# An LSTM with a residual on one core: GpSimd's output sums split in two, Strassen sums moved into the step, and the start of the x projection rewritten

## The chip, the cores and the metric

The kernel runs on one core of a Trainium2 chip. The metric is device time in microseconds (us) from the start of the program to its end. Five engines work side by side, each from its own queue, in the order in which the program lists its instructions: PE (TensorE, matrix products into PSUM), PEld (PE's loads of weights), DVE (VectorE), ACT (ScalarE) and POOL (GpSimd). SP starts DMAs. An engine waits for another by semaphores.

## The reference

The input x has 16 sequences of 512 steps with 512 features. The recurrence and the residual are:

```
xW = x @ Wx + b                        # Wx: 512 x 2048
a = xW[t] + h @ Wh                     # Wh: 512 x 2048, h0 given, c0 = 0
i, f, o = sigmoid(a[:512], a[512:1024], a[1024:1536]);  g = tanh(a[1536:])
c = f * c + i * g;   h = o * tanh(c)
out[:, t] = x[:, t] + h
```

All is in 32-bit floats; each of the 512 steps needs the h of the step before.

## The kernel before, in words

**Layout.** The four column blocks j of 32 units lie on the four groups of 32 partitions. A pair of steps q shares a tile: 32 columns are two steps of 16 sequences. The hidden units are two halves, a and b, with a PSUM bank each (`gates`, two per half, taken in turn by even and odd steps). Each loop step t computes `products` on PE, h @ Wh for the step, in 16-bit floats: Wh is three 16-bit pieces, wq0 to wq2, and h is stored in `parts` as a main part, a scaled remainder and their copies. STEP_PE lists the order: the digit is the piece, the first letter the half of h that is read, the second the half of the gates that is written. It is 96 matmuls of 256 columns in groups of four (one for each j). In one group of four the four run side by side.

**One step.** After its products, STEP gives the order of the small operations on DVE and ACT, for half a and half b: `turn` and `turno` (L378, a transpose from PSUM), `fold` and `foldo` (L385, adds the remainder's part), `act`, `sigo`, `scale` (ACT), `mix` (L417), `cell` (L423), `ctanh` (ACT, L427), then p1 (L444, the main part of the new h), h (L433, h itself into `hist`), rem (L452), p2 (L448) and p2r (L456, the remainders). q3 of STEP_PE needs p1 alone, q1 needs p2, q2 needs p2r. Two steps ahead, `seed` (L330, ACT) writes bias and x part from the bank `xb` into the gates of step t + 2, times a mask that selects the step of the pair.

**The x part.** It is made in two ways. For pairs q below 2*M0 (M0 = 6) `turn_x` (L218) transposes the x block into x^T and writes a half of it, `xH`; `project` (L226) multiplies by Wx in eight fp32 matmuls of 256 columns per chunk, with `xH` for the sigmoid gates' columns (the kernel uses tanh for a sigmoid, so these gates need a factor of 0.5) and x^T for the others. From m = M0 on, four steps at a time (m = t // 4 or so) go by Strassen's scheme: `turn_set` (L238) transposes two pairs into XT, `sum_x` (L255) makes the sums 5, 7, 6 and 3 of blocks of x^T, one after each step at t % 4 = 3, 0, 1, 2; `strassen` (L274) multiplies them with sums of blocks of Wx, four lists of units in PHASES, and `add_side` (L296), `copy_side`, `copy_first`, `bias_main` and `bias_side` combine the banks. The sums of Wx are made once, by `sum_w` (L303), two pieces after each of the steps 1 to 16; they hold a factor of 0.5 for the sigmoid gates' blocks. `arrived` (L208) is a small copy, made for the first pair of each block of 16 steps, that waits for all DMAs of this block of x.

**The output.** At t % 4 = 2 `residual` (L489) transposes two pairs of `hs` (h without its scale) to `hb`, and GpSimd adds x to them into `ob` in one instruction of 128x256 (L497); at the end of each block of 16 steps `put` issues 32 DMAs on SP, and `load_xs` 32 loads at the step with ti == 3. The last block's pairs are written one by one by `put_pair`.

The few lines that set the order around the change:

```python
STEP = (
    ...
    "p1_b h_b rem_b p2_b p2r_b"
)
...
M0 = 6
...
        if r == 3:
            ...
            if M0 <= (t + 9) // 4 < NM:
                turn_set((t + 9) // 4)
                sum_x((t + 9) // 4, 5)
```

Of the kernel before, what the change touches and what calls it, by code (L numbers as in the profile page):

```python
# [7 lines left out]
FP = mybir.dt.float32  # L8
HP = mybir.dt.float16
# [6 lines left out]
Q = 32  # L16
# [7 lines left out]
STEP = (  # L24
    "turn_a turno_a fold_a act_a foldo_a sigo_a turn_b scale_a mix_a turno_b cell_a ctanh_a "
    "fold_b act_b foldo_b sigo_b p1_a scale_b h_a mix_b p2_a cell_b ctanh_b rem_a p2r_a "
    "p1_b h_b rem_b p2_b p2r_b"
)

LAST = (  # L30
# [1 line left out]
    "mix_a sigo_b cell_a ctanh_a mix_b cell_b ctanh_b h_a h_b"  # L32
)

M0 = 6
PHASES = (
    "1:0 1:1 5:0 5:1l",
    "5:1r 6:0 6:1 2:0",
# [19 lines left out]
def lstm_residual(ctx: ExitStack, tc: tile.TileContext, x, h0, wx, wh, b, out):  # L58
# [74 lines left out]
        w.rearrange("p k (g h c j u) -> p k h j g c u", g=G, h=2, c=2, j=NJ) for w in wq  # L133
    ]
    bias = const.tile([P, G * P], FP, tag="bias", name="bias")
    mask = const.tile([P, S2], FP, tag="mask", name="mask")
    zero = const.tile([1, G * P], HP, tag="zero", name="zero")
    amax = const.tile([P, 8], FP, tag="amax", name="amax")
    top = const.tile([P, 2], FP, tag="top", name="top")
# [14 lines left out]
    FIRST_SLOT = ((1, 3, 0), (0, 3, 1))  # L154
    SLOTS = ((1, 2, 4), (1, 0, 3))
    last_h = const.tile([P, S2, NK, Q], FP, tag="last_h", name="last_h")
    last_o = const.tile([P, S2, P], FP, tag="last_o", name="last_o")
    parts = [
        [const.tile([P, 2, 5, N], HP, tag=f"parts{h}{i}", name=f"parts{h}{i}") for i in range(2)]
# [39 lines left out]
                    )  # L199


    xT, xH, XT, XS = {}, {}, {}, {}
    summed, side = {}, {}

    def put_bias(q):
# [12 lines left out]
    def turn_x(q):  # L218
        s, i = divmod(q, XP)
        arrived(q)  # L220
        pair = xtp.tile([P, 2, NK, Q], FP, tag="XT", name=f"xT_{q}")
        xT[q], xH[q] = pair[:, 0], pair[:, 1]
        nc.vector.transpose(xT[q].rearrange("p c m -> p (c m)"), xs[s][:, i])
        nc.vector.tensor_scalar(xH[q], xT[q], 0.5, None, ALU.mult)

    def project(q, c):  # L226
        for e in range(2):
            for j in range(NJ):
                nc.tensor.matmul(  # L229
                    xb[q % NXB][j * Q : (j + 1) * Q, (1 - e) * GU : (2 - e) * GU],  # L230
                    lhsT=(xT if e else xH)[q][:, c],
                    rhs=wx_j[:, c, j, 2 * (1 - e) : 2 * (2 - e)],
                    start=False,
                    stop=False,
                    skip_group_check=True,
                )

    def turn_set(m):  # L238
        s, i = divmod(2 * m, XP)
        arrived(2 * m)  # L240
        XT[m] = xtp.tile([P, 2, NK, Q], FP, tag="XT", name=f"XT_{m}")
        XS[m] = xtp.tile([P, 4, 2, Q], FP, tag="XS", name=f"XS_{m}", bufs=2)
        nc.vector.transpose(
            XT[m].rearrange("p a c m -> p (a c m)"),
            xs[s][:, i : i + 2].rearrange("p i f -> p (i f)"),
        )
# [80 lines left out]
    def x_bank(q):  # L327
        return xb[2 if q >= 2 * M0 and q % 2 == 0 else q % NXB]

    def seed(t, h):  # L330
        nc.scalar.mul(  # L331
            gates[h][t % 2][:, :GU].rearrange("p (g u) -> p g u", g=G),
            x_bank(t // 2).rearrange("p (g h u) -> p h g u", g=G, h=2)[:, h],
            mask[:, t % 2 : t % 2 + 1],
        )


    def products(t, i, kh, h, chunks):
        g = gates[h][t % 2]
# [12 lines left out]
    def first_products(c):  # L352
        for e in range(2):
            for j in range(NJ):
                nc.tensor.matmul(
                    xb[0][j * Q : (j + 1) * Q, (1 - e) * GU : (2 - e) * GU],
                    lhsT=(hT0 if e else hH0)[:, c],
                    rhs=wh_j[:, c, e, j],
                    start=False,
                    stop=False,  # L360
                    skip_group_check=True,
                )
# [31 lines left out]
    def slots(t, h, kind):  # L394

        return parts[h][(t + 1) % 2][:, :, SLOTS[(t + 1) % 2][kind]]
# [89 lines left out]
                    in_=ob[s][p0 : p0 + N, i].rearrange("p (c u) -> p c u", c=NK),  # L486
                )

    def residual(p, n):  # L489
        s, i = divmod(p, XP)  # L490
        if i == 0:
            ob[s] = outp.tile([P, XP, P], FP, tag="ob", name=f"ob_{s}")
        hb = work.tile([P, n, P], FP, tag=f"hb{n}", name=f"hb_{p}", bufs=n)
        nc.vector.transpose(  # L494
            hb.rearrange("p i f -> p (i f)"), hs[p].rearrange("p i c m -> p (i c m)")
        )
        nc.gpsimd.tensor_tensor(ob[s][:, i : i + n], hb, xs[s][:, i : i + n], ALU.add)  # L497
        if s == NS - 1:
            for k in range(i, i + n):
                put_pair(s, k)  # L500
        elif i + n == XP:
            put(s)

    def last_sum(r):
# [16 lines left out]
    hH0 = work.tile([P, NK, Q], FP, tag="hH0", name="hH0", bufs=1)  # L521
# [3 lines left out]
    halves = const.tile([1, Q], FP, tag="halves", name="halves")  # L525
    bias_d = const.tile([P, GU], FP, tag="bias_d", name="bias_d")
    for e in range(2):
        nc.scalar.dma_start(
# [7 lines left out]
    nc.vector.memset(amax, 0.0)  # L536
    nc.vector.memset(h_in, 0.0)
    nc.vector.memset(ones, 1.0)
    nc.vector.memset(halves, 0.5)
    nc.gpsimd.memset(neg, 0.0)  # L540
    nc.gpsimd.affine_select(
        out=neg,
# [26 lines left out]
    for j in range(NJ):  # L569
        nc.vector.memset(mask[j * Q : j * Q + N, 0:1], 1.0)  # L570
    nc.vector.tensor_scalar(mask[:, 1:2], mask[:, 0:1], -1.0, 1.0, ALU.mult, ALU.add)
    for h in range(2):
        for i in range(2):
            nc.vector.memset(parts[h][i], 0.0)
# [11 lines left out]
    for bank in xb:  # L586
        for e in range(2):
            for j in range(NJ):
                nc.tensor.matmul(
                    bank[j * Q : (j + 1) * Q, (1 - e) * GU : (2 - e) * GU],  # L590
                    lhsT=ones if e else halves,
                    rhs=brow[e].rearrange("p (g c j u) -> p j g c u", g=2, c=NK, j=NJ)[:, j],
                    start=(e == 0),
                    stop=False,
                    skip_group_check=True,
                )
# [88 lines left out]
    def start(op, a="", b=""):  # L685
        if op == "b":
            bound(a, b == "s")
        elif op == "S":
            scales(int(a))
        elif op == "hT":  # L690
            nc.vector.transpose(hT0.rearrange("p c m -> p (c m)"), h_in)
            nc.vector.tensor_scalar(hH0, hT0, 0.5, None, ALU.mult)
        elif op == "xT":
            turn_x(int(a))
        elif op == "H":
            first_products(int(a))
        elif op == "P":
            project(int(a), int(b))
        elif op == "seed":
            seed(int(a), int(b))  # L700
        elif "_" in op:
            name, h = op.split("_")
            act(0, name, "ab".index(h))
        else:
            split(op, int(a), b == "s")
# [4 lines left out]
    load_xs(2)  # L710

    NM = T // 4
    CHUNKS = {"": range(2), ".": range(1), ",": range(1, 2)}
    for t in range(1, T):
        s, ti = divmod(t, XB)
# [12 lines left out]
        if M0 <= m < NM:  # L728
            for unit in PHASES[ph].split():
                strassen(m, int(unit[0]), int(unit[2]), unit[3:])  # L730

        for op in (STEP if t + 1 < T else LAST).split():
            name, h = op.split("_")
            act(t, name, "ab".index(h))

# [5 lines left out]
        if t == T - 3:  # L741
            for h in range(2):
                unscale(t // 2, 1, h)
            residual(t // 2, 1)
# [10 lines left out]
        if t == 17:  # L755
            nc.vector.tensor_tensor(bias_d, bias[:, GU:], bias[:, :GU], ALU.subtract)
        if t <= 16:
            sum_w(2 * t - 2)
            sum_w(2 * t - 1)
        r = t % 4  # L760
        if r == 3:
            if M0 <= (t + 5) // 4 < NM:
                copy_first((t + 5) // 4)
            if M0 <= (t + 9) // 4 < NM:
                turn_set((t + 9) // 4)
                sum_x((t + 9) // 4, 5)
            if t + 1 < T - 3:
                unscale(t // 2 - 1, 2, 0)
        elif r == 0:
            if M0 <= (t + 4) // 4 < NM:  # L770
                add_side((t + 4) // 4, 3)
            if M0 <= (t + 8) // 4 < NM:
                sum_x((t + 8) // 4, 7)
            if t > 0:
                unscale(t // 2 - 2, 2, 1)
            if t == T - 4:
                residual(t // 2 - 2, 2)
        elif r == 1:
            if M0 <= (t + 3) // 4 < NM:
                add_side((t + 3) // 4, 8)  # L780
            if M0 <= (t + 7) // 4 < NM:
                sum_x((t + 7) // 4, 6)
                bias_main((t + 7) // 4)
        else:
            if M0 <= (t + 6) // 4 < NM:
                sum_x((t + 6) // 4, 3)
                bias_side((t + 6) // 4)
            if 4 < t < T - 4:
                residual(t // 2 - 3, 2)
        if ti == 3 and s + 2 < NS:  # L790
            load_xs(s + 2)

# [27 lines left out]
```

## Time and profile before

| what | us |
|---|---|
| median of 3 runs | 2226.73 (2226.35 to 2226.89) |
| the profiled execution | 2227.05 |
| its span in the trace | 2225.2 |
| first `turn_a` of step 0, from the span's start | 32.5 |
| `turn_a` of step 1 to that of step 28 | 126.7 |
| `turn_a` of step 28 to that of step 508 | 2036.4 |
| from `turn_a` of step 511 to the end of the span | 9.8 |

Profiled operations that the change touches, mean time of one: `sum_x` 128x64 0.216 to 0.221 us; sums of Wx 128x256 0.42; `hb` 128x256 0.438; GpSimd's add of 128x256 0.730, of 128x128 0.456; `turn_x` 0.305 and its half 0.228; a seed 0.437; a matmul of `project` 0.380 (fp32 matmuls are two records each).

How to read the profile: a row of the groups gives line, engine, operation, output<-input tiles, shape and count, then busy us and mean ns of one, then the engine's idle time before it and who ended it. Times in one engine's timeline overlap, since an operation starts before the one before it has ended; so the step from one start to the next is what an operation costs, not its duration. A matmul's end is modelled; its start is recorded. The chain of waits gives start, us and the work that the end of the program hung on.

### The profile page before, as it was taken

How to read it: one execution, taken by the hardware profiler on the slowest of the kernel's cores; microseconds unless marked ns; L12 is line 12 of the kernel's file. 1: busy time of each engine (PE TensorE's matmuls, PEld its weight loads, DVE VectorE, ACT ScalarE, POOL GpSimd, SP SyncE). 2: the span in 40 equal slices, each digit the busy share in tenths (PEclk: the TensorE clock that was granted, in tenths of full speed). 3: DMA queues.
4: the chain of work that ended last, by engine and by line, in shares of the span. 5: the costliest groups of instructions: out<-in, count | busy, mean ns of one | idle time of the engine just before them, and what ended most of it. 6: DMA issues, size and time to landing. Idle time of an engine off the chain costs nothing.

```text
span 2225.2 us, 152487 instructions
## 1 busy us (share of the span) xinstructions
PE 2187.3 (98%) x65604; PEld 1658.1 (75%) x65604; DVE 2113.4 (95%) x12392; ACT 1573.2 (71%) x5910; POOL 109.6 (5%) x164
## 2 busy tenths in 40 slices
PE   9999999999999999999999999999999999999997
PEld 5677777777777777777777777777777777777775
DVE  7999999999999999999999999999999999999998
ACT  6667777777777777777777777777777777777775
POOL 2000000000000000000000000000000000000000
PEclk9999999999999999999999999999999999999999
DMA  5111111111111111111111111111111111111101
GB/s 167 28 22 17 19 18 23 23 19 17 18 21 24 22 19 17 18 23 23 20 17 18 19 23 23 17 17 18 22 23 20 19 17 19 23 23 17 18 8 21
DMA packets 302505, 52.39 MB, mean 24 GB/s; under 512 B 299330, under 2 KB 299778, under 8 KB 301828
## 3 DMA queue, kind: packets, MB, share of 16 engines
q1 hardware_dynamic: 300768, 42.39, 12.5%
q8 instruction: 512, 8.39, 1.6%
q14 instruction: 165, 1.35, 0.2%
q0 software_dynamic: 896, 0.23, 0.1%
q10 hardware_dynamic: 164, 0.02, 0.0%
HBM read 25.73 MB, written 16.78 MB: 19 GB/s over the span
## 4 chain that ended last, share of the span: by engine, by line
PE 29%; DVE 23%; issue 21%; SPq 21%; DMA 4%; POOL 2%; ACT 1%; DVEq 0%; POOLq 0%
PE gates L343 21%; SPq L475 18%; PE xb L278 8%; DVE gt L378 5%; DMA out_dram<-ob 3%; SPq L184 3%; DVE pre L385 2%; DVE parts L444 2%; DVE gto L378 2%; POOL ob L497 2%; DVE pr L417 2%; DVE parts L456 1%; DVE hb L494 1%; DVE preo L385 1%; DVE rem L452 1%
## 5 line engine op out<-in xcount | busy, mean ns | idle before, releaser
L343 PE MATMUL gates<-wq,parts 128*32 128x256 f16 x49056 | 1434.5, 273 | 26.8 <-DVE parts L444 18.6
L343 PEld LDWEIGHTS <-parts 128*32 128x32 f16 x49056 | 1166.5, 96 | 290.4 <-DVE parts L444 152.7
L411 ACT ACTIVATE gc<-pre 128x96 f32<-128x96 f32 x1022 | 289.6, 283 | 534.6 <-DVE pre L385 534.6
L331 ACT ACTIVATE gates<-xb,mask 128x256 f32<-128x256 f32 x1024 | 409.1, 437 | 0.9 <-PE xb L229 0.9
L378 DVE STREAM_TRANSPOSE gt<-gates 128x192 f32<-128x192 f32 x1024 | 388.6, 380 | 17.1 <-PE gates L343 4.0
L278 PE MATMUL xb<-sums,XS 128*32 128x256 f32 (+1 forms) x6832 | 380.2, 349 | 0.0
L415 ACT ACTIVATE os<-so,sc 128x32 f32<-128x32 f32 x1022 | 328.8, 322 | 33.2
L278 PEld LDWEIGHTS xb<-sums,XS 128*32 128x32 f32 x6832 | 201.5, 110 | 116.7
L385 DVE SCALAR_TENSOR_TENSOR pre<-gt 128x96 f32<-128x96 f32 x1024 | 279.1, 273 | 0.0
L427 ACT ACTIVATE tch<-gc 128x32 f32<-128x32 f32 x1024 | 234.9, 229 | 57.0
L278 PE MATMUL xb<-wx_sb,XT 128*32 128x256 f32 x3904 | 274.0, 379 | 0.0
L444 DVE TENSOR_TENSOR parts<-os,tch 128x64 f16<-128x64 f32 x1022 | 230.8, 226 | 12.6
L456 DVE SCALAR_TENSOR_TENSOR parts<-rem,parts 128x32 f16<-128x32 f32 x1022 | 197.1, 193 | 35.5
L378 DVE STREAM_TRANSPOSE gto<-gates 128x64 f32<-128x64 f32 x1024 | 229.8, 224 | 0.0
L413 ACT ACTIVATE so<-preo 128x32 f32<-128x32 f32 x1024 | 217.9, 213 | 0.4 <-DVE preo L385 0.3
L417 DVE SCALAR_TENSOR_TENSOR pr<-gc 128x64 f32<-128x64 f32 x1022 | 213.7, 209 | 0.0
L452 DVE SCALAR_TENSOR_TENSOR rem<-parts,hist 128x32 f32<-128x32 f16 x1022 | 192.3, 188 | 17.7
L497 POOL TENSOR_TENSOR ob<-hb,xs 128x256 f32<-128x256 f32 x128 | 93.1, 727 | 2096.3 <-DVE hb L494 1738.8
L385 DVE SCALAR_TENSOR_TENSOR preo<-gto 128x32 f32<-128x32 f32 x1024 | 188.6, 184 | 0.0
L448 DVE SCALAR_TENSOR_TENSOR parts<-parts,hist 128x32 f16<-128x32 f16 x1022 | 188.5, 184 | 0.0
L433 DVE SCALAR_TENSOR_TENSOR hist<-os,tch 128x32 f32<-128x32 f32 x1022 | 188.5, 184 | 0.0
L423 DVE SCALAR_TENSOR_TENSOR gc<-pr 128x32 f32<-128x32 f32 x1024 | 174.9, 171 | 0.1
(97 smaller groups left out, 1348.7 us busy)
## 6 DMA issues: line engine op xcount, KB each, us to landing
xs<-in_x_dram SPq DMA_DIRECT2D x1024, 16.0 KB, 2.6
out_dram<-ob SPq DMA_DIRECT2D x992, 16.0 KB, 2.2
wh_sb<-in_L_cond_Wh_dram SPq DMA_DIRECT2D x8, 512.0 KB, 7.8
wx_sb<-in_L_cond_Wx_dram SPq DMA_DIRECT2D x8, 512.0 KB, 12.4
out_dram<-ob SPq DMA_DIRECT2D x56, 8.0 KB, 1.5
xs<-in_x_dram SPq DMA_DIRECT2D x40, 8.0 KB, 2.6
xs<-in_x_dram POOLq DMA_DIRECT2D x24, 8.0 KB, 5.7
out_dram<-last_o SPq DMA_DIRECT2D x6, 8.0 KB, 1.5
```

Source lines behind the costliest of these rows:

```text
L278: nc.tensor.matmul(region(m, k)[j * Q : (j + 1) * Q, g.start * P : g.stop * P], lhsT=left(m, k, i), rhs=w[:, j, g], start=False, stop=Fals ...
L331: nc.scalar.mul(gates[h][t % 2][:, :GU].rearrange("p (g u) -> p g u", g=G), x_bank(t // 2).rearrange("p (g h u) -> p h g u", g=G, h=2)[:, ...
L343: nc.tensor.matmul(g[j * Q : (j + 1) * Q, :GU], lhsT=parts[kh][t % 2][:, cc, k : k + 2].rearrange("p k n -> p (k n)"), rhs=wq_j[i - 1][:, ...
L378: nc.vector.transpose(gt.rearrange("p b m -> p (b m)"), gates[h][t % 2][:, b0 * Q : b1 * Q])
L385: nc.vector.scalar_tensor_tensor(pre.rearrange("p g (c n) -> p (g c) n", c=2), gt[:, :, (1 - t % 2) * N : (2 - t % 2) * N], 1.0 / LO, gt[: ...
L411: nc.scalar.activation(gc[h][:, 0:3], v["pre", h], AF.Tanh)
L415: nc.scalar.mul(new("os", t, h, [P, 2 * N]), v["so", h], S[h])
L417: nc.vector.scalar_tensor_tensor(new("pr", t, h, [P, 2, 2 * N]), gc[h][:, 1:3], 1.0, gc[h][:, ::3], ALU.add, ALU.mult)
L427: nc.scalar.activation(new("tch", t, h, [P, 2 * N]), gc[h][:, 3], AF.Tanh, scale=0.5)
L444: nc.vector.tensor_tensor(parts[h][(t + 1) % 2][:, :, 1 : k + 2 : k], twice[0], twice[1], ALU.mult)
L456: nc.vector.scalar_tensor_tensor(slots(t, h, 2), v["rem", h], 2.0, slots(t, h, 1), ALU.mult, ALU.subtract)
L475: nc.sync.dma_start(out=out_j[j, :, s * XB + r : (s + 1) * XB : S2, c], in_=ob[s][p0 : p0 + N, :, c * Q : (c + 1) * Q],)
```

## The change

It has these parts:

- **GpSimd's sums.** `residual` no longer adds. It queues its one or two pairs in a list, and `add_next` takes one pair from it: one add of 128x128. The first is made at t % 4 = 2, right after the transpose; the second at t % 4 = 3, behind a one-element copy on GpSimd that reads what `p2r_b` of this step wrote. `put` and `put_pair` follow the adds. At t = T - 4 both are made at once.
- **Sums of x^T blocks.** `sum_x` moves from the step's end into STEP, between `h_b` and `rem_b`. They come a step later than before: 5, 7, 6, 3 at t % 4 = 0, 1, 2, 3. `turn_set` no longer calls `arrived`; that is made three steps earlier, at t % 4 = 0.
- **Start of the x projection.** M0 is 8 in place of 6, so 32 steps in place of 24 go by direct products. `sum_w`'s 32 pieces are spread over the steps 1 to 26, one a step and two at t % 4 = 0. `bias_d` is made at t = 25 and not at 17.
- **Half weights by the mask.** `xH`, `hH0` and `halves` go. `project` is four matmuls of 512 columns per chunk. The bank holds full sums, and the first 32 steps' seeds are two ACT instructions of 128 columns each, one with the mask, one with half the mask. From step 32 on a seed is one instruction as before.

```diff
 STEP = (
...
-    "p1_b h_b rem_b p2_b p2r_b"
+    "p1_b h_b sum rem_b p2_b p2r_b"
 )
-M0 = 6
+M0 = 8
...
-    mask = const.tile([P, S2], FP, tag="mask", name="mask")
+    mask = const.tile([P, 2 * S2], FP, tag="mask", name="mask")
...
-        pair = xtp.tile([P, 2, NK, Q], FP, tag="XT", name=f"xT_{q}")
-        xT[q], xH[q] = pair[:, 0], pair[:, 1]
+        xT[q] = xtp.tile([P, 2, NK, Q], FP, tag="XT", name=f"xT_{q}")[:, 0]
         nc.vector.transpose(xT[q].rearrange("p c m -> p (c m)"), xs[s][:, i])
-        nc.vector.tensor_scalar(xH[q], xT[q], 0.5, None, ALU.mult)
 
     def project(q, c):
-        for e in range(2):
-            for j in range(NJ):
-                nc.tensor.matmul(
-                    xb[q % NXB][j * Q : (j + 1) * Q, (1 - e) * GU : (2 - e) * GU],
-                    lhsT=(xT if e else xH)[q][:, c],
-                    rhs=wx_j[:, c, j, 2 * (1 - e) : 2 * (2 - e)],
...
+        for j in range(NJ):
+            nc.tensor.matmul(
+                xb[q % NXB][j * Q : (j + 1) * Q],
+                lhsT=xT[q][:, c],
+                rhs=wx_j[:, c, j],
...
     def turn_set(m):
         s, i = divmod(2 * m, XP)
-        arrived(2 * m)
...
     def seed(t, h):
...
+        out = gates[h][t % 2][:, :GU].rearrange("p (g u) -> p g u", g=G)
+        x = x_bank(t // 2).rearrange("p (g h u) -> p h g u", g=G, h=2)[:, h]
+        if t < 4 * M0:
+            nc.scalar.mul(out[:, :2], x[:, :2], mask[:, t % 2 : t % 2 + 1])
+            nc.scalar.mul(out[:, 2:], x[:, 2:], mask[:, 2 + t % 2 : 3 + t % 2])
+        else:
+            nc.scalar.mul(out, x, mask[:, t % 2 : t % 2 + 1])
...
-                    lhsT=(hT0 if e else hH0)[:, c],
+                    lhsT=hT0[:, c],
...
-        nc.gpsimd.tensor_tensor(ob[s][:, i : i + n], hb, xs[s][:, i : i + n], ALU.add)
+        for k in range(n):
+            sums.append((s, i + k, hb[:, k]))
+        add_next()
+        if t == T - 4:
+            add_next()
+
+    def add_next():
+        s, i, hb = sums.pop(0)
+        nc.gpsimd.tensor_tensor(ob[s][:, i], hb, xs[s][:, i], ALU.add)
         if s == NS - 1:
-            for k in range(i, i + n):
-                put_pair(s, k)
-        elif i + n == XP:
+            put_pair(s, i)
+        elif i == XP - 1:
             put(s)
...
+        m = (t + (8, 7, 6, 5)[t % 4]) // 4
         for op in (STEP if t + 1 < T else LAST).split():
+            if op == "sum":
+                if M0 <= m < NM:
+                    sum_x(m, (5, 7, 6, 3)[t % 4])
+                continue
...
-        if t <= 16:
-            sum_w(2 * t - 2)
-            sum_w(2 * t - 1)
+        if t <= 26:
+            for _ in range(2 - (t % 4 > 0)):
+                if pieces:
+                    sum_w(pieces.pop(0))
         r = t % 4
         if r == 3:
...
                 turn_set((t + 9) // 4)
-                sum_x((t + 9) // 4, 5)
             if t + 1 < T - 3:
                 unscale(t // 2 - 1, 2, 0)
+            if sums:
+                nc.gpsimd.tensor_copy(ready, slots(t, 1, 2)[0:1, 0, 0:1])
+                add_next()
         elif r == 0:
             if M0 <= (t + 4) // 4 < NM:
                 add_side((t + 4) // 4, 3)
-            if M0 <= (t + 8) // 4 < NM:
-                sum_x((t + 8) // 4, 7)
+            if M0 <= (t + 12) // 4 < NM:
+                arrived((t + 12) // 2)
...
```

At t % 4 = 1 and 2 the calls of `sum_x` go in the same way.

More of the change, by code (lines that the diff above doesn't have):

```diff
@@ L156, in lstm_residual @@
     last_h = const.tile([P, S2, NK, Q], FP, tag="last_h", name="last_h")
+    ready = const.tile([1, 1], HP, tag="ready", name="ready")
     last_o = const.tile([P, S2, P], FP, tag="last_o", name="last_o")
@@ L199, in load_first @@
                     )
-    xT, xH, XT, XS = {}, {}, {}, {}
+    xT, XT, XS = {}, {}, {}
     summed, side = {}, {}
@@ L220, in turn_x @@
         arrived(q)
-        pair = xtp.tile([P, 2, NK, Q], FP, tag="XT", name=f"xT_{q}")
-        xT[q], xH[q] = pair[:, 0], pair[:, 1]
+        xT[q] = xtp.tile([P, 2, NK, Q], FP, tag="XT", name=f"xT_{q}")[:, 0]
         nc.vector.transpose(xT[q].rearrange("p c m -> p (c m)"), xs[s][:, i])
-        nc.vector.tensor_scalar(xH[q], xT[q], 0.5, None, ALU.mult)
     def project(q, c):
-        for e in range(2):
-            for j in range(NJ):
-                nc.tensor.matmul(
-                    xb[q % NXB][j * Q : (j + 1) * Q, (1 - e) * GU : (2 - e) * GU],
-                    lhsT=(xT if e else xH)[q][:, c],
-                    rhs=wx_j[:, c, j, 2 * (1 - e) : 2 * (2 - e)],
[L233 to L236, printed above, removed]
+        for j in range(NJ):
[3 more added lines that the diff above has]
+                rhs=wx_j[:, c, j],
+                start=False,
+                stop=False,
+                skip_group_check=True,
+            )
     def turn_set(m):
         s, i = divmod(2 * m, XP)
-        arrived(2 * m)
         XT[m] = xtp.tile([P, 2, NK, Q], FP, tag="XT", name=f"XT_{m}")
@@ L330, in seed @@
     def seed(t, h):
[L331 to L335, printed above, removed]
+        out = gates[h][t % 2][:, :GU].rearrange("p (g u) -> p g u", g=G)
[5 more added lines that the diff above has]
+            nc.scalar.mul(out, x, mask[:, t % 2 : t % 2 + 1])
     def products(t, i, kh, h, chunks):
@@ L487, in put_pair, with residual @@
                 )
-    def residual(p, n):
+    sums = []
+    def residual(t, p, n):
         s, i = divmod(p, XP)
@@ L520, in lstm_residual @@
     hT0 = work.tile([P, NK, Q], FP, tag="hT0", name="hT0", bufs=1)
-    hH0 = work.tile([P, NK, Q], FP, tag="hH0", name="hH0", bufs=1)
     warm = const.tile([1, 1], FP, tag="warm", name="warm")
@@ L524, in lstm_residual @@
     ones = const.tile([1, Q], FP, tag="ones", name="ones")
-    halves = const.tile([1, Q], FP, tag="halves", name="halves")
     bias_d = const.tile([P, GU], FP, tag="bias_d", name="bias_d")
@@ L538, in lstm_residual @@
     nc.vector.memset(ones, 1.0)
-    nc.vector.memset(halves, 0.5)
     nc.gpsimd.memset(neg, 0.0)
@@ L571, in lstm_residual @@
     nc.vector.tensor_scalar(mask[:, 1:2], mask[:, 0:1], -1.0, 1.0, ALU.mult, ALU.add)
+    nc.vector.tensor_scalar(mask[:, 2:4], mask[:, 0:2], 0.5, None, ALU.mult)
     for h in range(2):
@@ L590, in lstm_residual @@
                     bank[j * Q : (j + 1) * Q, (1 - e) * GU : (2 - e) * GU],
-                    lhsT=ones if e else halves,
+                    lhsT=ones,
                     rhs=brow[e].rearrange("p (g c j u) -> p j g c u", g=2, c=NK, j=NJ)[:, j],
@@ L691, in start @@
             nc.vector.transpose(hT0.rearrange("p c m -> p (c m)"), h_in)
-            nc.vector.tensor_scalar(hH0, hT0, 0.5, None, ALU.mult)
         elif op == "xT":
@@ L712, in lstm_residual @@
     NM = T // 4
+    pieces = list(range(32))
     CHUNKS = {"": range(2), ".": range(1), ",": range(1, 2)}
@@ L743, in lstm_residual @@
                 unscale(t // 2, 1, h)
-            residual(t // 2, 1)
+            residual(t, t // 2, 1)
         elif t == T - 2:
@@ L754, in lstm_residual @@
             turn_x(q + 1)
-        if t == 17:
-            nc.vector.tensor_tensor(bias_d, bias[:, GU:], bias[:, :GU], ALU.subtract)
-        if t <= 16:
-            sum_w(2 * t - 2)
-            sum_w(2 * t - 1)
+        if t == 4 * M0 - 7:
+            nc.vector.scalar_tensor_tensor(
+                bias_d, bias[:, GU:], 0.5, bias[:, :GU], ALU.mult, ALU.subtract
+            )
+        if t <= 26:
+            for _ in range(2 - (t % 4 > 0)):
+                if pieces:
+                    sum_w(pieces.pop(0))
         r = t % 4
@@ L776, in lstm_residual @@
             if t == T - 4:
-                residual(t // 2 - 2, 2)
+                residual(t, t // 2 - 2, 2)
         elif r == 1:
@@ L781, in lstm_residual @@
             if M0 <= (t + 7) // 4 < NM:
-                sum_x((t + 7) // 4, 6)
                 bias_main((t + 7) // 4)
@@ L785, in lstm_residual @@
             if M0 <= (t + 6) // 4 < NM:
-                sum_x((t + 6) // 4, 3)
                 bias_side((t + 6) // 4)
             if 4 < t < T - 4:
-                residual(t // 2 - 3, 2)
+                residual(t, t // 2 - 3, 2)
         if ti == 3 and s + 2 < NS:
```

## The prediction

> **What bounds the kernel now.** I read the page first, then the chain of waits, then the timeline of VectorE and of the weight loads inside single steps. The page says only that two engines are nearly full:
>
> ```profile
> PE 2187.3 (98%) x65604; PEld 1658.1 (75%) x65604; DVE 2113.4 (95%) x12392; ACT 1573.2 (71%) x5910; POOL 109.6 (5%) x164
> ...
> L343 PEld LDWEIGHTS <-parts 128*32 128x32 f16 x49056 | 1166.5, 96 | 290.4 <-DVE parts L444 152.7
> ```
>
> The second line shows that PE's weight loads do run dry, waiting for p1 (L444). To see a step's length I take the start of every second 192-column transpose (L378, `turn_a`) as the mark of a step. Steps 28 to 507 then fall into three kinds: 359 of mean 4.156 us, 92 of 4.406 and 29 of 4.800; together 2036.4 us. All that are not 4.156 have t % 4 = 3. The chain of waits (start, us, what) shows what a 4.156 step is:
>
> ```profile
> 1002.35 1.51 PE xb L278 x32
> 1003.87 1.91 PE gates L343 x68
> 1005.80 0.38 DVE gt L378
> ```
>
> and the timeline (of VectorE, and a later line of GpSimd) what is odd in the long one:
>
> ```profile
> 1009.50 0.44 DVE L494 STREAM_TRANSPOSE hb<-hs 128x256 f32<-128x256 f32 x1
> 1009.96 0.38 DVE L378 STREAM_TRANSPOSE gt<-gates 128x192 f32<-128x192 f32 x1
> 1010.27 0.21 DVE L378 STREAM_TRANSPOSE gto<-gates 128x64 f32<-128x64 f32 x1
> 1010.40 0.47 DVE L385 SCALAR_TENSOR_TENSOR pre<-gt 128x96 f32<-128x96 f32 x1
> ...
> 1026.89 0.73 POOL L497 TENSOR_TENSOR ob<-hb,xs 128x256 f32<-128x256 f32 x1 [16.14 <-DMA out_dram<-ob]
> ```
>
> First reading: `turn_a` is released from within a step's 96 products, by the last of half a's, which STEP_PE puts into the 19th of 24 groups of four. So the loop is turn_a, then VectorE and ScalarE up to p1_a, then PE's first 19 groups, then the next turn_a. Step 246 in numbers from its turn_a: p1_a ends at 2.008, the first product starts 0.054 later, groups follow each 0.109, turn_a comes at 4.163. PE itself is not far behind: 24 groups x 0.109 = 2.62 and 1.51 of x work make 4.13; its last x matmul leaves only 12 to 24 ns of slack. So 4.14 is a floor.
>
> Second reading: the fold of 1010.40 takes 0.47 us, where the same line takes 0.24 in other steps. GpSimd's add starts 79 ns after the end of `hb` in every one of 128 cases and takes 0.73, so it covers this fold each fourth step. From turn_a to p1_a that step needs 2.010 us instead of 1.785: 0.225 lost. (The 16.14 us is only GpSimd's idle time; with 79 ns everywhere no add waited for an output DMA.)
>
> Third reading, the end of a step on VectorE and the weight load that needs it:
>
> ```profile
> 1088.32 0.19 DVE L433 SCALAR_TENSOR_TENSOR hist<-os,tch 128x32 f32<-128x32 f32 x1
> 1088.43 0.22 DVE L417 SCALAR_TENSOR_TENSOR pr<-gc 128x64 f32<-128x64 f32 x1
> 1088.56 0.19 DVE L448 SCALAR_TENSOR_TENSOR parts<-parts,hist 128x32 f16<-128x32 f16 x1
> ...
> 1089.31 0.18 DVE L433 SCALAR_TENSOR_TENSOR hist<-os,tch 128x32 f32<-128x32 f32 x1
> 1089.53 0.19 DVE L452 SCALAR_TENSOR_TENSOR rem<-parts,hist 128x32 f32<-128x32 f16 x1
> 1089.64 0.18 DVE L448 SCALAR_TENSOR_TENSOR parts<-parts,hist 128x32 f16<-128x32 f16 x1
> 1089.86 0.20 DVE L456 SCALAR_TENSOR_TENSOR parts<-rem,parts 128x32 f16<-128x32 f32 x1
> ...
> 1090.11 0.10 PEld L343 LDWEIGHTS <-parts 128*32 128x32 f16 x4
> ```
>
> p2r_b (L456) ends at 1090.053, its weights load 52 ns later, and the group after it starts 118 ns behind the last instead of 109: the b half's tail has no slack left, 0 to 8 ns.
>
> **Part by part.**
>
> *GpSimd's add in two.* The 128x128 add has rows: 456 ns (L497, last pair) and 457 (L509). The first half starts 79 ns after `hb` and ends 535 ns after it. With the sum gone from in front of it, `hb` (natural step 0.365, from 438 - 75 of overlap) starts 3.58 after the last turn_a and ends near 4.02; the add ends at 4.56; the next turn_a comes at 4.17 and its fold 0.438 later, at 4.61. So the fold is clear, by some 50 ns. The second half is queued in step t % 4 = 3 behind a one-element copy that reads p2r_b's output. From that end (3.67): 0.08 to start, about 0.10 for the copy (a 128x1 fill on POOL took 98 to 101 ns), 0.05 between, 0.456: done by 4.36, beside `XT`'s transpose and turn_a, which ran at their usual 0.38 beside the old add too. What it adds: 126 copies on an engine that is 5% busy, and a wait of p2r_b two steps later for that copy; 8 us lie between, nothing queues. DMAs of `put` come one step (4 us) later and `load_xs` behind them on SP; the load's data are first read 17 steps after its issue (some 70 us), and 64 issues take about 30 us, so this costs nothing while that cover of 40 us holds. Gain: 0.225 on each of some 120 steps.
>
> *`arrived` moved to t % 4 = 0.* In 29 steps it costs 4.800 - 4.406 = 0.394: three semaphore instructions 96 ns apart, then the copy (107). Behind `add_side` (0.334 to the next start) the three run while that executes, so 3.58 + 0.33 + 0.11 = 4.02, hidden under turn_a's wait to 4.17. If they do not overlap, 4.31, 0.13 x 29 = 4 us back.
>
> *`sum_x` into the step, between h_b and rem_b.* It leaves the step's end, where t % 4 = 0 and 1 were waiting for PE anyway (its next start came 0.258 later, 0.135 where nothing was waited for): nothing gained there. At t % 4 = 3 it stood behind `XT` (0.472 + 0.143 = 0.615); without it and the collision that step is PE's loop again. New cost: in the a half h_a, mix, p2_a start 0.102 and 0.135 apart, mix being 64 columns of two inputs like the sum. So rem_b would start 0.237 after h_b; now it starts 0.219 after, held by h_b's own result. The tail p2_b, p2r_b comes 0.018 later, and as it has no slack the loop does: 4.156 + 0.018 = 4.174. Ends for this: 0 (if the next group of weights absorbs it; the floor of 4.14 excludes a gain beyond 0.015) and 0.22 (if the sum is run as a step of its own between two dependent ones). I take 0.018, because the a half has the very pattern. The sum needs no semaphore at three of its four old places.
>
> The Trainium skill, page "VectorE: DVE Perf Modes", section "The DRAIN you can't avoid", speaks against this part: it says that the next VectorE operation does not start until the pipe of the one before has emptied. By it the sum would add its whole 220 ns, some 480 x 0.2 = 96 us, and the change would lose; by the row, starts 0.102 apart where one operation takes 0.184, it adds 0.018. I go by the row.
>
> *Steady part:* 480 steps x 4.174 = 2003.5 against 2036.4: -32.9 us.
>
> *M0 from 6 to 8, x^T without the half, sums of Wx over 26 steps.* Now steps 1 to 27 take 126.7 us, most of them 4.5 to 5.5: VectorE there carries two 420 ns sums of Wx (next start 0.336) and, each second step, `xH` (0.15). One step, t = 19, holds both forms of x work and takes 5.86. After: no `xH`, one sum a step (two at t % 4 = 0). VectorE: 3.57 + 0.23 (xT) + 0.34 = 4.14, or 3.57 + 0.67 = 4.24, or 3.57 + 0.34 + 0.365 = 4.27. PE becomes the bound: 2.62 + 4 units of 0.431 + 0.011 = 4.36, for 27 steps (eight more than now at four units rather than three and a half). Matmuls of 512 columns keep the columns, so I count no gain there; half as many weight loads is off the path, since loads overlap. 27 x 4.36 = 117.6; the double step moves to t = 27, +1.5; ACT's half at t = 8 stands in front of the second sum, +0.6; `arrived` at t = 11 and the second add beside sums of Wx (0.1 x 5), +0.9. Sum 120.6: -6 us. The seeds of t < 32 become two activations. From 437 ns at 256 columns and 589 at 512 (L331, L206) I estimate 0.33 each, start to start 0.25, so +0.29 per step on ACT: seeds end near 3.65, put_bias and hs fill to 4.6, the next act_a is at 5.07: hidden, but with t % 4 = 0 the thinnest cover, some 0.3; without it up to 0.2 x 8.
>
> *Ends.* Before step 0 the seeds stand on the path (turn_a waited 0.76 for L331): +0.2, against 0.15 for `xH` and 0.1 for `hH`. At the tail two adds in a row collide differently: from -0.3 to +0.4. I count 0.
>
> *Sum.* 2225.2 - 32.9 - 6 = 2186.3 span. The profiled execution took 2227.05, 1.85 more than its span; so 2188.2, and as it lay 0.3 over the median of 2226.73, **2188 us**.
>
> **Rivals.**
> - *The sum vanishes in the bubble* (the tail's 18 ns are absorbed): 480 x 4.156, 2179, and with the early steps better than I count, 2174. For it: slack of 0 to 8 ns already in some steps. Against: the 118 ns spacing. Chance 0.12.
> - *A collision stays, or the sum is dearer* (0.05 a step, or one half add still meets a two-input operation for 0.1 to 0.2 each fourth step): 2188 + 480 x 0.03 = 2202, or + 120 x 0.2 = 2212. For it: cover of the fold is 50 ns. Chance 0.16.
> - *Slower:* the sum between two dependent operations costs as a step of its own, 0.22, on p2r_b's path in each step. The loop is 4.37, 480 x 4.37 = 2098, time about 2282. It decides from 0.09 a step: 480 x 0.09 = 43 us, about what the collision (27), `arrived` (11) and the early steps (6) give. Against it: 0.102 spacings throughout. Chance 0.07.
> - *GpSimd's split does not do what it says*, the add keeps delaying a fold by 0.225 at one of its places: 2188 + 27 = 2215 by the first half alone; with the dearer sum near no change. Chance of ending within 0.2%: 0.04.
>
> **How the numbers follow.** The forecast has 0.61, its own range 2181 to 2196. A measurement of this kernel can tell about 0.2% from no change. Faster: 0.61 + 0.12 + 0.16 = 0.89; same 0.04; slower 0.07. The range reaches from inside the bubble case to the middle of the dearer one: 2176 to 2207.
>
> **What would show it.** In the changed profile: L385's `pre` at one length, 0.24 to 0.25, in all steps; POOL with two adds of 0.456, neither over a fold; step lengths of one kind, 4.17; rem_b 0.237 behind h_b; no 4.8 steps; early steps of 4.36. Wrong would make it: rem_b later than 0.3 behind h_b, a `pre` over 0.3, p2r_b waiting for POOL, or ACT late in early steps.

## The result and the profile after

The changed kernel takes 2194.45 us (median of 4 runs, 2193.91 to 2194.81), the kernel before 2226.54 on the same chip: 0.9856 of it, 95% interval 0.9839 to 0.9873. Forecast were 2188 and 2176 to 2207. The profiled execution took 2193.91, its span 2192.1. Where the time went, by the marks of `turn_a`:

| stretch | before, us | after, us | forecast difference | difference |
|---|---|---|---|---|
| start to `turn_a` of step 1 | 39.34 | 40.49 | 0 | +1.15 |
| steps 1 to 27 | 126.70 | 119.35 | -6 | -7.35 |
| steps 28 to 507 | 2036.44 | 2009.42 | -32.9 | -27.0 |
| from step 508 to the end | 22.75 | 22.86 | 0 | +0.1 |

In steps 33 to 499 the means for t % 4 = 0, 1, 2, 3 are 4.171, 4.240, 4.167 and 4.167 us; before they were 4.151, 4.159, 4.158 and 4.504. So the long step is gone, three kinds stand at 4.167, and a new one has come, at t % 4 = 1. Three lines of the page of before that the prediction did not show, the engines' shares of the chain that ended last, the transposes and the fold:

```profile
PE 29%; DVE 23%; issue 21%; SPq 21%; DMA 4%; POOL 2%; ACT 1%; DVEq 0%; POOLq 0%
...
L378 DVE STREAM_TRANSPOSE gt<-gates 128x192 f32<-128x192 f32 x1024 | 388.6, 380 | 17.1 <-PE gates L343 4.0
...
L385 DVE SCALAR_TENSOR_TENSOR pre<-gt 128x96 f32<-128x96 f32 x1024 | 279.1, 273 | 0.0
```

The page of the changed kernel (line numbers have shifted: L383 is the fold, L442 p1, L376 the transposes):

```profile
PE 2174.1 (99%) x65092; PEld 1645.6 (75%) x65092; DVE 2035.4 (93%) x12369; ACT 1587.8 (72%) x5970; POOL 150.2 (7%) x417
...
PE 97%; DVE 1%; ACT 1%; DMA 0%; issue 0%; SPq 0%; ACTq 0%; POOL 0%; DVEq 0%; POOLq 0%
...
L341 PEld LDWEIGHTS <-parts 128*32 128x32 f16 x49056 | 1170.1, 96 | 263.9 <-DVE parts L442 100.7
...
L376 DVE STREAM_TRANSPOSE gt<-gates 128x192 f32<-128x192 f32 x1024 | 391.6, 382 | 78.9 <-PE gates L341 76.2
...
L383 DVE SCALAR_TENSOR_TENSOR pre<-gt 128x96 f32<-128x96 f32 x1024 | 247.6, 242 | 0.0
```

The mean fold is 242 ns (273 before). VectorE now waits for PE at `turn_a`, 76.2 us in all where it was 4.0, and the chain that ended last is 97% PE (29% before, where 21% of it ran through SP's DMA issues as well). The timeline of GpSimd shows the two adds in one group of four steps, and that of VectorE the fold beside the first:

```profile
473.98 0.46 POOL L505 TENSOR_TENSOR ob<-hb,xs 128x128 f32<-128x128 f32 x1 [12.28 <-DVE hb L494]
477.85 0.18 POOL L782 COPY ready<-parts 1x1 f16<-1x1 f16 x1 [3.41 <-DVE parts L454]
477.98 0.45 POOL L505 TENSOR_TENSOR ob<-hb,xs 128x128 f32<-128x128 f32 x1
```

```profile
472.80 0.18 DVE L431 SCALAR_TENSOR_TENSOR hist<-os,tch 128x32 f32<-128x32 f32 x1
472.90 0.22 DVE L257 TENSOR_TENSOR XS<-XS,XT 128x64 f32<-128x64 f32 x1
473.03 0.18 DVE L450 SCALAR_TENSOR_TENSOR rem<-parts,hist 128x32 f32<-128x32 f16 x1
473.14 0.18 DVE L446 SCALAR_TENSOR_TENSOR parts<-parts,hist 128x32 f16<-128x32 f16 x1
473.35 0.19 DVE L454 SCALAR_TENSOR_TENSOR parts<-rem,parts 128x32 f16<-128x32 f32 x1
473.46 0.44 DVE L494 STREAM_TRANSPOSE hb<-hs 128x256 f32<-128x256 f32 x1
474.06 0.38 DVE L376 STREAM_TRANSPOSE gt<-gates 128x192 f32<-128x192 f32 x1 [0.15 <-PE gates L341]
474.36 0.20 DVE L376 STREAM_TRANSPOSE gto<-gates 128x64 f32<-128x64 f32 x1
474.49 0.24 DVE L383 SCALAR_TENSOR_TENSOR pre<-gt 128x96 f32<-128x96 f32 x1
```

The first add ends at 474.44, the fold starts at 474.49. The sum (L257) stands between h_b and rem_b, 0.102 behind the one and 0.135 ahead of the other, and p2 follows rem_b by 0.102. The same stretch of VectorE in a step with t % 4 = 1, from 468.90:

```profile
468.90 0.18 DVE L446 SCALAR_TENSOR_TENSOR parts<-parts,hist 128x32 f16<-128x32 f16 x1
469.19 0.19 DVE L454 SCALAR_TENSOR_TENSOR parts<-rem,parts 128x32 f16<-128x32 f32 x1
469.30 0.42 DVE L294 TENSOR_TENSOR xb<-xb,side 128x256 f32<-128x256 f32 x1
469.89 0.38 DVE L376 STREAM_TRANSPOSE gt<-gates 128x192 f32<-128x192 f32 x1 [0.17 <-PE gates L341]
```

Here p2r_b starts 0.29 behind p2_b and not 0.22. Its record waits for a semaphore of GpSimd too, and in this kind of step alone a semaphore instruction of VectorE's queue, 21 ns long, stands 66 ns ahead of it.

### The profile page after: what moved, and what is told of

Read it like the earlier page. It is cut to its first block, busy times and chain, and to the rows that moved or that the text cites. A ratio compares the mean times of both kernels' runs of the same rounds, so it can differ in the third digit from the quotient of the medians.

```text
span 2192.1 us, 152010 instructions
## 1 busy us (share of the span) xinstructions
PE 2174.1 (99%) x65092; PEld 1645.6 (75%) x65092; DVE 2035.4 (93%) x12369; ACT 1587.8 (72%) x5970; POOL 150.2 (7%) x417
## 4 chain that ended last, share of the span: by engine, by line
PE 97%; DVE 1%; ACT 1%; DMA 0%; issue 0%; SPq 0%; ACTq 0%; POOL 0%; DVEq 0%; POOLq 0%
PE gates L341 61%; PE xb L275 33%; PE xb L227 2%; PE gates L662 0%; DVE gt L376 0%; PE xb L594 0%; PE xb L353 0%; ACT tch L425 0%; DMA brow<-in_L_cond_b_dram 0%; DVE gto L376 0%; DVE parts L442 0%; DVE pr L415 0%; SPq L473 0%; DVE pre L383 0%; ACT gates L334 0%
## 5 line engine op out<-in xcount | busy, mean ns | idle before, releaser
L376 DVE STREAM_TRANSPOSE gt<-gates 128x192 f32<-128x192 f32 x1024 | 391.6, 382 | 78.9 <-PE gates L341 76.2
L334 ACT ACTIVATE gates<-xb,mask 128x256 f32<-128x256 f32 x960 | 384.2, 438 | 0.0
L275 PE MATMUL xb<-sums,XS 128*32 128x256 f32 (+1 forms) x6720 | 373.8, 349 | 0.0
L275 PE MATMUL xb<-wx_sb,XT 128*32 128x256 f32 x3840 | 269.5, 379 | 0.0
L383 DVE SCALAR_TENSOR_TENSOR pre<-gt 128x96 f32<-128x96 f32 x1024 | 247.6, 242 | 0.0
L442 DVE TENSOR_TENSOR parts<-os,tch 128x64 f16<-128x64 f32 x1022 | 230.1, 225 | 13.0
L376 DVE STREAM_TRANSPOSE gto<-gates 128x64 f32<-128x64 f32 x1024 | 227.5, 222 | 0.0
L505 POOL TENSOR_TENSOR ob<-hb,xs 128x128 f32<-128x128 f32 x255 | 115.6, 454 | 1594.2 <-DVE hb L494 1494.7
L415 DVE SCALAR_TENSOR_TENSOR pr<-gc 128x64 f32<-128x64 f32 x1022 | 205.5, 201 | 0.0
L450 DVE SCALAR_TENSOR_TENSOR rem<-parts,hist 128x32 f32<-128x32 f16 x1022 | 187.3, 183 | 1.0
L383 DVE SCALAR_TENSOR_TENSOR preo<-gto 128x32 f32<-128x32 f32 x1024 | 187.4, 183 | 0.0
```

The lines of the kernel that those rows point to most:

```text
L275: nc.tensor.matmul(region(m, k)[j * Q : (j + 1) * Q, g.start * P : g.stop * P], lhsT=left(m, k, i), rhs=w[:, j, g], start=False, stop=Fals ...
L334: nc.scalar.mul(out, x, mask[:, t % 2 : t % 2 + 1])
L376: nc.vector.transpose(gt.rearrange("p b m -> p (b m)"), gates[h][t % 2][:, b0 * Q : b1 * Q])
L383: nc.vector.scalar_tensor_tensor(pre.rearrange("p g (c n) -> p (g c) n", c=2), gt[:, :, (1 - t % 2) * N : (2 - t % 2) * N], 1.0 / LO, gt[: ...
L415: nc.vector.scalar_tensor_tensor(new("pr", t, h, [P, 2, 2 * N]), gc[h][:, 1:3], 1.0, gc[h][:, ::3], ALU.add, ALU.mult)
L442: nc.vector.tensor_tensor(parts[h][(t + 1) % 2][:, :, 1 : k + 2 : k], twice[0], twice[1], ALU.mult)
```

## The experiments

The theory: a GpSimd add holds a VectorE operation with two SBUF inputs that starts under it, so that it can't end before the add has; VectorE's tail p2_b, p2r_b has no slack, so each delay in it lengthens the step; the rest of the step's end is covered by PE. The main rivals: the split pays by itself; or the sums' place does, or neither adds to the other. All are timed against the kernel before on their own chip, and totals are given as ratios to it. The chips themselves differ: the kernel before took 2226.5 us on the chip of the result, 2228.5 on that of the first four runs below, 2229.3 on that of the next four and 2227.0 on that of the last three. So two stretches of some 2010 us from different chips can differ by 2 us or more with no cause in the kernels; there I compare kinds of step within one trace.

### Split alone

The kernel before with `residual` and `add_next` of the changed one, the copy and the second half add at t % 4 = 3.

```diff
-        nc.gpsimd.tensor_tensor(ob[s][:, i : i + n], hb, xs[s][:, i : i + n], ALU.add)
+        for k in range(n):
+            sums.append((s, i + k, hb[:, k]))
+        add_next()
...
+            if sums:
+                nc.gpsimd.tensor_copy(zero[:, 0:1], slots(t, 1, 2)[0:1, 0, 0:1])
+                add_next()
```

> The kernel before with GpSimd's add in two halves alone, the second behind the copy that reads p2r_b's output. My theory (a GpSimd add delays a VectorE operation with two SBUF inputs that it overlaps): the first half ends about 4.68 after the step's turn_a and the next fold begins at 4.59, so that fold is nearly free, but the second half (3.90 to 4.35) now lies over sum 5 behind the transpose of XT (from 4.04), which is held to its end: steps with t % 4 = 3 stay near 4.40. The copy's wait at p2r_b adds 0.07 at t % 4 = 1. Steps 28 to 508 about 2036, total about 2227, no gain. Rival (the split is what pays, by itself): 0.225 x 120 = 27 us less, about 2200.

Measured: 0.9996 (0.9987 to 1.0005) of the kernel before, steps 28 to 507 2037.6 us. No gain. The timeline of VectorE at the end of such a step, then GpSimd's:

```profile
469.98 0.44 DVE L243 STREAM_TRANSPOSE XT<-xs 128x256 f32<-128x256 f32 x1
470.45 0.42 DVE L260 TENSOR_TENSOR XS<-XT 128x64 f32<-128x64 f32 x1
470.78 0.37 DVE L378 STREAM_TRANSPOSE gt<-gates 128x192 f32<-128x192 f32 x1
```

```profile
470.32 0.45 POOL L507 TENSOR_TENSOR ob<-hb,xs 128x128 f32<-128x128 f32 x1
```

The fold is free in this kernel, but the second half add lies over sum 5, which takes 0.42 in place of 0.22: 4.38 for this step (median). The collision has changed its victim. The transpose of XT beside the same add keeps its 0.44.

### Sums alone

The kernel before with `sum` in STEP and the four `sum_x` calls at the step's end removed.

```diff
-    "p1_b h_b rem_b p2_b p2r_b"
+    "p1_b h_b sum rem_b p2_b p2r_b"
```

> The kernel before with the four sums of x^T blocks moved between h_b and rem_b alone. My theory: steps of 4.167, and with hb 0.135 earlier the add of 0.73 overlaps the fold less: its end at 4.83 against the fold's start at 4.605 leaves a delay of about 0.11 in place of 0.236, so steps with t % 4 = 3 take 4.28, and about 4.45 in the 29 with the copy of arrived. Steps 28 to 508 about 2018, total about 2209. Rival (the split is what pays; the sums only trade places): 2225 to 2232.

Measured: 0.9902 (0.9887 to 0.9917), steps 28 to 507 2017.6 us, t % 4 = 3 at 4.27 (median). So this part alone gives some 20 us (18.8 by the two traces, and this chip is the slower by 2), though it takes no work away: with the sum gone from in front of `hb`, the unsplit add starts 0.13 earlier against the step, and the fold takes 0.33 in place of 0.47:

```profile
479.74 0.33 DVE L385 SCALAR_TENSOR_TENSOR pre<-gt 128x96 f32<-128x96 f32 x1
479.99 0.18 DVE L385 SCALAR_TENSOR_TENSOR preo<-gto 128x32 f32<-128x32 f32 x1
```

### The change without the split

One add of 128x256 behind `hb`, no copy; all else as in the changed kernel.

> The changed kernel with one GpSimd add of 128x256 behind hb, no copy. My theory: the fold of the step with t % 4 = 3 is delayed by about 0.11, and t % 4 = 1 wins back the 0.073 of the copy's wait: (3 x 4.167 + 4.28) / 4 = 4.195 a step, steps 28 to 508 about 2014, total about 2199. Rival (the split pays its 27 us whatever else is there): 2194.5 + 27 - 9 = 2212.

Measured: 0.9864 (0.9849 to 0.9878), steps 28 to 507 2013.8 us, t % 4 = 3 at 4.263, t % 4 = 1 at 4.170. The intervals of the totals can't tell this kernel from the changed one, and the traces come from different chips. Within each trace, against its other kinds of step: here t % 4 = 3 is 0.09 longer, some 11 us in 120 steps; in the changed kernel t % 4 = 1 is 0.07 longer, 8.6 us. So the split is worth 11 us in the change, its copy takes back 8.6, and some 2 are left.

### The change without the copy

```diff
-                nc.gpsimd.tensor_copy(ready, slots(t, 1, 2)[0:1, 0, 0:1])
```

> The changed kernel without GpSimd's one-element copy: the second half add is queued at the same place but may run as soon as the first is done, from 4.58 to 5.02 after a step's turn_a, over the next fold at 4.605. My theory: that fold is held by about 0.3, t % 4 = 3 takes about 4.47, while t % 4 = 1 falls to 4.167: total 2194.5 - 9 + 36, about 2222. Rival (halves are short enough, the copy only costs its wait): about 2186.

Measured: 0.9934 (0.9917 to 0.9950), t % 4 = 3 at 4.407, t % 4 = 1 at 4.171. Both adds run at once, and the fold pays, VectorE's line first:

```profile
476.91 0.48 DVE L383 SCALAR_TENSOR_TENSOR pre<-gt 128x96 f32<-128x96 f32 x1
```

```profile
476.40 0.88 POOL L505 TENSOR_TENSOR ob<-hb,xs 128x128 f32<-128x128 f32 x2 [16.04 <-DVE hb L494]
```

I had put the delay at 0.30; it is 0.24, since the second add starts 43 ns before the first has ended, and the pair took 0.88, not 0.91 and a gap. The copy is needed, but this run also shows that t % 4 = 1 falls to 4.171 without it.

### A copy that reads another tile

The copy keeps its place, but reads a one-element tile that VectorE fills in the same step, rather than p2r_b's output.

```diff
+    def mark(t):
+        flag[0] = work.tile([1, 1], HP, tag="flag", name=f"flag_{t}")
+        nc.vector.memset(flag[0], 0.0)
...
         if r == 3:
+            if sums:
+                mark(t)
...
-                nc.gpsimd.tensor_copy(ready, slots(t, 1, 2)[0:1, 0, 0:1])
+                nc.gpsimd.tensor_copy(ready, flag[0])
```

> The changed kernel, in which GpSimd's one-element copy reads a one-element tile that VectorE fills right behind p2r_b, instead of p2r_b's own output. My theory: the extra 0.073 of p2r_b at t % 4 = 1 is the second wait, on GpSimd, that the copy's reading lays on the p2r_b two steps later; without it all four kinds of step take 4.167, 120 x 0.073 = 8.8 us less: about 2185.7. Rival (the 0.073 comes from something else in these steps, such as ACT's copies or add_side): 2194.5, p2r_b at t % 4 = 1 still 0.29 behind p2_b.

Measured: 0.9814 (0.9800 to 0.9829), all four kinds of step within 4.170 to 4.175, steps 28 to 507 2002.6 us. p2r_b stands 0.22 behind p2_b in a step with t % 4 = 1 too:

```profile
466.65 0.18 DVE L446 SCALAR_TENSOR_TENSOR parts<-parts,hist 128x32 f16<-128x32 f16 x1
466.87 0.19 DVE L454 SCALAR_TENSOR_TENSOR parts<-rem,parts 128x32 f16<-128x32 f32 x1
```

So the 0.073 was the second wait that the copy's reading laid on p2r_b: the semaphore instruction ahead of it is gone too, and add_side stands in its place as before. The run without the copy had shown 4.171 here as well.

### The sums back at the step's end

The kernel of the last run, with each sum behind p2r_b (t % 4 = 0 and 1), behind `hb` (2) or ahead of XT's transpose (3).

```diff
-    "p1_b h_b sum rem_b p2_b p2r_b"
+    "p1_b h_b rem_b p2_b p2r_b"
...
         if r == 3:
             if sums:
                 mark(t)
+            late_sum(t)
...
                 residual(t, t // 2 - 3, 2)
+            late_sum(t)
```

> The kernel flag with the four sums put back to the end of the step: behind p2r_b at t % 4 = 0 and 1, behind hb at 2, ahead of the transpose of XT at 3. My theory: the step's end has 0.22 to 0.26 of cover, so the sum of 0.135 is free there, while in the step it costs 0.011: steps of 4.156, 480 x 0.011 = 5 us less than flag, about 2180.5. Rival (VectorE's step end is the bound and the place in the step is what made room): more than flag, 2190 or over.

Measured: 0.9793 (0.9779 to 0.9808), 2183.18 us; steps of 4.162, steps 28 to 507 1997.95 us, 4.6 less than with the sums in the step on the same chip. It is faster than both kernels. So it was not the place between h_b and rem_b that gained; that place costs 0.010 a step. What gained was that no sum stands ahead of `hb` or behind XT any more. The four were moved together, so the share of each was not measured. What the place costs shows in PE's products, by the median of the trace's matmul starts: a group of four starts 109 ns behind the one before, and with the sums in the step two groups that read the b half's p2 and p2r start 116 to 120 and 116 to 117 behind, here 109 and 114 to 115. With its other two late starts (11 to 13 ns each, in both kernels) PE waits here for less than 30 ns a step: PE is the bound.

### `arrived` back in `turn_set`

> The changed kernel with the copy of arrived back in turn_set at t % 4 = 3. My theory: VectorE then reaches the next turn_a at 3.58 + 0.39 + 0.365 = 4.34 in place of 4.167 in 29 steps, 5 us more: about 2199.5. Rival (it is hidden there as well, and its 0.39 in the kernel before came only from the sum and the collision behind it): 2194.5.

Measured: 0.9871 (0.9855 to 0.9888), steps 28 to 507 2014.5 us, 5.1 more than in the changed kernel, but on a slower chip: here all other kinds of step are some 0.005 longer too, 2 us in all. Within this trace the steps with `arrived` take 4.31 (median) where others with t % 4 = 3 take 4.172, and the step behind each takes 4.127 and wins 0.045 back. That is some 0.1 in each of 29, about 3 us, not the 5 expected. At t % 4 = 0 its waits are hidden, but for the steps 132 and 292, which take 4.40 in the changed kernel.

### The start as before

> The changed kernel with the start of the kernel before: M0 = 6, x^T with its half, matmuls of 256 columns, one instruction a seed, two sums of Wx after each of the steps 1 to 16. My theory: steps 1 to 28 go back from 119.4 to about 126, and the time up to step 1 falls by 1.1 (no seeds in two): about 2194.5 + 6 = 2200.5. Rival (the early steps gain nothing, the difference is made up by the longer span of direct products): 2193 to 2195.

Measured: 0.9880 (0.9866 to 0.9895), steps 1 to 27 125.9 us, start 38.85. The new start gives 6 to 6.5 us in steps 1 to 27 (119.35 to 119.9 in the runs that have it) and takes back 0.24 in step 0, which is 6.87 long here and 7.11 there; the rest of the difference ahead of step 1 is within what the start varies by between runs of one start. The other 0.8 of the 7.35 in steps 1 to 27 came with the parts for the steady steps: in the kernel before, the folds of t = 7, 11, 15, 19, 23 and 27 took 0.47 to 0.61 under an add, here three take 0.33 to 0.34.

### The control, the sums of Wx two a step, and the half weights back

The changed kernel again, as a control on this chip: 0.9852 (0.9837 to 0.9866), steps 1 to 27 119.34 us.

> The changed kernel as it is, beside the next two on one chip. All theories: 0.985 to 0.986 of the kernel before; steps 1 to 28 119.4 us, up to step 1 about 40.

```diff
-        if t <= 26:
-            for _ in range(2 - (t % 4 > 0)):
-                if pieces:
-                    sum_w(pieces.pop(0))
+        if t <= 16:
+            for _ in range(2):
+                sum_w(pieces.pop(0))
```

> The changed kernel with the sums of Wx made two a step after steps 1 to 16, as before, and nothing else undone. My theory: in those steps VectorE needs 3.57 + 0.23 + 0.67 = 4.47 in odd steps, 4.60 with hb, against PE's 4.34; steps 17 to 27 stay at PE's 4.34. Steps 1 to 28 rise by about 2 to 3 us. Rival (the spread is the whole gain of the early steps): they rise by 6.

Measured: 0.9890 (0.9874 to 0.9907), steps 1 to 27 126.74 us, 7.4 more. My sum failed here and the rival holds. It lacked that the second sum of a step needs the first's result, or, in the first eight steps, ACT's half, which now stands behind four seed instructions and, in even steps, put_bias. The waits for that half come to 3.8 us here and to 0.9 in the changed kernel; the rest was not taken apart. At t = 8 the timeline of VectorE has

```profile
78.98 0.42 DVE L318 SCALAR_TENSOR_TENSOR sums<-wx_sb,half 128x256 f32<-128x256 f32 x1 [0.87 <-ACT half L315]
```

> The kernel sum_end with x^T's half, matmuls of 256 columns and one instruction a seed, as before; M0 = 8 and the spread sums stay. My theory: with one sum a step VectorE needs 3.57 + 0.23 + 0.15 + 0.34 = 4.29 and still hides behind PE's 4.34, so steps 1 to 28 stay within 0.5 of sum_end's 119.6, and the time up to step 1 falls by about 1.2 with the single seeds: 0.5 to 1.5 us less than sum_end. Rival (the half weights by the mask are a part of the early gain): steps 1 to 28 rise by 2 or more.

Measured: 0.9801 (0.9786 to 0.9815), steps 1 to 27 121.94 us, 2.3 more than with the half by the mask; up to step 1 39.67 against 39.74. The rival's number holds, but its cause only in part. x^T's half waits for the transpose (a step of 0.34 for xT rather than 0.23), so VectorE needs some 4.40 in odd steps, over PE's 4.34. That also brings the collision back: VectorE's step end comes later against the next step, `hb` and the fill of the flag with it, and so do GpSimd's adds. Eight early folds lie under an add here and together lose some 1 us, where the run it was made from has one (0.3 us). VectorE's line first:

```profile
107.20 0.43 DVE L389 SCALAR_TENSOR_TENSOR pre<-gt 128x96 f32<-128x96 f32 x1
```

```profile
107.06 0.45 POOL L516 TENSOR_TENSOR ob<-hb,xs 128x128 f32<-128x128 f32 x1
```

Half, matmuls and seeds were put back together, and the flag lies in another tile in this run, so 2.3 us is no price of the half alone. In total it can't be told from the kernel it was made from.

## Why the prediction was right, point by point

- **The collision of add and fold**, 0.225 on some 120 steps: right as a mechanism. With the fold free the long step is 4.167; without the copy a single fold of 0.48 brings back 0.24. The Trainium skill, page "SBUF — State Buffer", section "Who interferes with whom", says that a VectorE instruction with two SBUF inputs contends with a GpSimd instruction that reads SBUF, and one with at most one does not, outside the modes in which VectorE uses both its ports. The runs agree: fold (0.47) and sum (0.42) were held, transposes beside the same adds kept 0.38 and 0.44. But the prediction booked these 27 us under the split, and the runs book them elsewhere. The split alone is worth nothing (0.9996): its second half only finds a free place because sum 5 has gone from behind XT. The sums' move alone is worth some 20 us, and the split with its copy adds some 2 to it.
- **`arrived`**: right in direction, about 3 us with its old place restored. The 29 x 0.394 = 11 us that I put on it hold for the kernel before, where VectorE was already late in those steps; with sum and collision gone from them the rest of the step covers most of it.
- **The sum in the step**: right mechanism, smaller size. rem_b stands 0.238 behind h_b, as reckoned; but it costs 0.011 a step and not 0.018, since p2 follows rem_b by 0.102 where it was 0.109, and 4.6 us in all by the run with the sums at the end. The section of the page "VectorE: DVE Perf Modes" that I set against it also says that a next operation that is not held starts earlier than the emptied pipe. So it does not speak against this part: starts 0.102 apart behind an operation of 0.185 are such a case, and 0.2 a step did not follow from it.
- **The copy on GpSimd**: this step failed. The prediction counts "a wait of p2r_b two steps later for that copy; 8 us lie between, nothing queues" and puts it at nothing. The wait was indeed long over, yet p2r_b now waits for two semaphores, and the second wait takes 0.073 in the one place with no slack: 120 x 0.073 = 8.8 us, shown by the run with the flag. "p2r_b waiting for POOL" stood among the signs of being wrong, and it came. The cover for the DMAs was smaller than reckoned as well (64 issues on SP take 41 us in the trace of before, not about 30); beyond a few single steps such as 132 and 292 the step lengths show no cost of it.
- **Steps 1 to 27**: -7.4, forecast -6. PE is the bound there as forecast (15 of the 27 steps take 4.32 to 4.36), but how the gain falls to the parts was not in the prediction: without the spread it is gone (+7.4), and with the half, its matmuls and single seeds back 2.3 of it is gone, part of that by collisions.
- **The ends**: I counted 0. Step 0 lengthens from 6.87 to 7.11 in all runs with two instructions a seed, +0.24 where I had +0.2 and about as much off. The start up to step 0 lay between 31.4 and 33.4 us over the runs, also between runs with the same start; what moves it was not tried.
- **A reading that was off**, with no price on it: the last of half a's products is the 17th of the 24 groups, not the 19th. The chain shows it, 68 matmuls ahead of `turn_a`. And two of the 92 steps of 4.406 have t % 4 = 0.
- **The sum** 2188 was 6.4 short. In the span +8.8 for the copy's wait, -0.007 x 480 = -3.4 for the cheaper sum, +0.5 for the steps 132 and 292, -1.4 early, +1.2 at the start and +0.1 at the end make the 5.8 measured; the profiled execution lay 0.5 under its median, where I had put it 0.3 over. That misses of both signs stand in this sum, so that it came out this near, is partly luck.

## What to carry to other kernels

In this kernel work on GpSimd was not free for VectorE: look which operation with two SBUF inputs starts under each add, and remember that shifting one operation by 0.13 us can decide it. Splitting the add only helps if there is a free place for each piece. And a second semaphore can cost time though it has long been signalled: take an ordering signal from a tile that nothing on the critical tail writes.

## What the runs showed of the hardware

- A fold held by GpSimd's add ends 115 ns after the add (medians 115 or 116 in four runs), whether it starts 0.22 us before the add's end (sums alone, no split) or 0.35 (before, no copy). The smaller sum ends 89 ns after it (split alone). A fold that starts 76 ns before the add's end is not held (split alone, 0.24).
- A second semaphore on p2r_b cost 0.073 us though GpSimd had given it about 8 us before; it put a semaphore instruction of its own into the queue.
- Two seeds of 128 columns into the same bank start 0.35 to 0.38 apart, where 0.25 had been reckoned from the slope of longer ones; the next pair's first, into another bank, comes 0.27 behind.
